# A two-layer graph network on one core: layer 0 in groups of up to eight pairs, its leaks taken from PSUM, its outputs summed by VectorE

## The chip, the core and the metric

The kernel runs on one core of a Trainium2 chip. The metric is the device time of one execution in microseconds (us), and lower is better. Three timed executions of the kernel before gave 8651.25, 8656.15 and 8656.24 us, so the median is 8656.15 us. A further execution was profiled and took 8639.11 us; all views of the profile belong to that one.

## What is computed

There are 12500 nodes with 64 features and 400000 edges, sorted by target. Two graph layers follow one another, each added to its input and normalised over the features:

```python
# layer 0, for every edge (src -> dst)
msg_in = concatenate([x[dst], x[src] - x[dst]], axis=-1)
h = leaky_relu(msg_in @ W1 + b1, 0.01)
h = leaky_relu(h @ W2 + b2, 0.01)
out = segment_sum(h, dst)
x = layernorm(x + out)
# layer 1: attention with 4 heads over the same edges (and self loops):
# softmax over the edges of a target, weighted sum of x[src] @ W, mean of the heads
x = layernorm(x + attention(x))
```

The first product of layer 0 splits: `x[dst] @ (W1a - W1b) + b1` depends on the target alone, and `x[src] @ W1b` on the source alone. Both are made once for every node, and an edge then costs one gathered row, an addition, a leak, a product with W2 and a second leak.

## The kernel before, in words

**Windows.** The nodes are sorted by degree and cut into 98 windows of 128 nodes, one node to a partition. Window w has room for `KW[w]` edges for each of its nodes, from 64 down to 19, 3180 slots in all. Every slot of a window is one indirect DMA issued by GpSimd (POOL), which fetches one table row for each of the 128 nodes: `gather_rows`, line 278. Layer 0 makes 3180 of them from `btab`, layer 1 makes 3180 from `t1tab`.

**Preparation.** Before that, the nodes pass in natural order through eight batches: six of 14 columns, one of 8 and one of 6. For each batch GpSimd gathers edge rows into `rt` (98 gathers, line 278), `Terms` makes the two products of each node and `Bins` counts the degrees. A batch is worked off in groups of up to four columns, and `in_step` (from line 565) writes the order out by hand: for step i it issues `turn` of group i (four PE transposes and a ScalarE copy to `xt`), `mark` of group i of the batch before (VectorE builds the one-hot `oh`, then PE products, line 522 to 529), `multiply` of the same group i (PE, line 498, then a VectorE addition, line 499, and two ScalarE copies, lines 503 and 504), and `place` of group i-1 (VectorE, lines 535 and 537). After the steps VectorE compares the edge rows (`lt`, line 590), reduces them and takes the degrees, which `degrees` also copies by ScalarE and sends out by a DMA of SP. The order of the source is the order on every engine (`manual_schedule`).

**Layer 0.** `fetch0` issues the gathers of window w+2 ahead of the work on window w; the tile `g` that they fill has five buffers. Two slots make a pair, so a window has `KW[w] // 2 + 1` pairs, 1663 in all. They are worked off in groups of up to four pairs, 453 groups, last pairs first. For a group, `expand` transposes the pairs on PE (line 878) into PSUM and VectorE adds the target's term into `ht` in SBUF (line 880). `leak` (line 884) is one VectorE instruction that reads `ht` from SBUF twice, once times 0.01, and keeps the larger. `second` multiplies with W2 (line 889) and ScalarE adds the bias into `t` in SBUF (line 891); `leak` again. `collect` adds the two halves of a pair by a PE product with `both` (line 898), accumulates the groups in PSUM, and VectorE reduces the last four columns (line 903). Then `norm` makes the window's rows and `logits` their attention terms, which SP writes to `t1tab` and `state`. The groups run in a pipeline that is written out: in iteration i the loop issues `second` of group i-2, `expand` and the first leak of group i, the second leak of group i-2, `collect` of group i-4, and `norm` and `logits` one and two iterations after a window's last `collect`.

**Index tables.** For every batch of up to seven windows `index_slots` builds the slot indices on VectorE (lines 249 to 275) out of rows `xab` that GpSimd has gathered.

**Layer 1** gathers from `t1tab`, so its first gather comes after the last window's rows have been written. It is not touched by the change.

The two lines that a sentence does not say exactly:

```python
            def leak(x):
                nc.vector.scalar_tensor_tensor(x, x, 0.01, x, op0=ALU.mult, op1=ALU.max)
```

Of the kernel before, what the change touches and what calls it, by code (L numbers as in the profile page):

```python
# [10 lines left out]
F32 = mybir.dt.float32  # L11
# [10 lines left out]
P = 128  # L22
D = 64
# [3 lines left out]
G = 8  # L27
# [35 lines left out]
def tile_gnn_resnorm(ctx: ExitStack, tc: tile.TileContext, x, src, dst, w1, b1, w2, b2,  # L63
# [397 lines left out]
    with tc.tile_pool(name="prep", bufs=1) as prep, \  # L461
# [19 lines left out]
        class Terms:  # L481
# [10 lines left out]
                nc.scalar.copy(self.xt[:, :n, :], pt[:, :n, :])  # L492

            def multiply(self):
                n, g0, g1 = self.n, self.g0, self.g1
                pab = pps2.tile([P, 4, 2 * D], F32, name="pab")
                for w in range(n):
                    nc.tensor.matmul(pab[:, w, :], self.xt[:, w, :], wab, start=True, stop=True)
                nc.vector.tensor_tensor(
                    self.rt[:, self.o:self.o + n, D:X0].rearrange("p w (a d) -> p w a d", a=2),  # L500
                    pab[:, :n, None, :D].to_broadcast([P, n, 2, D]),
                    b1_bc[:, None, None, :].to_broadcast([P, n, 2, D]), op=ALU.add)
                nc.scalar.copy(bt[0][:, g0:g1, 1:], pab[:, :n, D:])
                nc.scalar.copy(bt[1][:, g0:g1, :D], pab[:, :n, D:])
# [53 lines left out]

        def degrees(a, b):
            nc.vector.tensor_sub(deg[:, a:b], ptr[:, a + 1:b + 1], ptr[:, a:b])  # L560
            nc.scalar.copy(info[:, a:b, 1], deg[:, a:b])
            nc.scalar.copy(info[:, a:b, 2], ptr[:, a:b])
            nc.sync.dma_start(xtab_v[:, a:b, XL:], info[:, a:b, :])
            return [Bins(g, min(g + 4, b)) for g in range(a, b, 4)]

        def in_step(terms, bins):
            for i in range(max(len(terms), len(bins)) + 1):
                if i < len(terms):
                    terms[i].turn()
                if i < len(bins):  # L570
                    bins[i].mark()
                if i < len(terms):
                    terms[i].multiply()
                if 0 <= i - 1 < len(bins):
                    bins[i - 1].place()

        rts = [load_inputs(*batches[0]), load_inputs(*batches[1])]
        nc.vector.tensor_sub(wab[:, :D], w1a, wab[:, D:])
# [122 lines left out]
    with tc.tile_pool(name="l0", bufs=1) as l0:  # L701
# [131 lines left out]

        with tc.tile_pool(name="m0", bufs=2) as mp, \
                tc.tile_pool(name="m0_t", bufs=4) as tp, \
                tc.tile_pool(name="m0_h", bufs=4) as hp, \
                tc.tile_pool(name="m0_x", bufs=3) as xp, \
                tc.tile_pool(name="m0_g", bufs=5) as gp, \
                tc.tile_pool(name="m0_ps", bufs=2, space=PSUM) as mps, \
                tc.manual_schedule():  # L840
            per = G // 2
            raws, own = {}, {}

            def fetch0(w):
                if w in batches:
                    index_slots(mp, *raws[w])
                    own[w] = raws.pop(w)
                else:
                    own[w] = own.pop(w - 1)
                for b in batches[:-1]:  # L850
                    if b not in done and b <= w + 2:
                        done.add(b)
                        raws[b] = load_rows(xp, b)
                k = KW[w]
                xa = own[w][2][:, w - own[w][0], :]

                g = gp.tile([P, KMAX // 2 + 1, 2 * DB], F32, name="g")
                nc.vector.memset(g[:, k // 2, (k % 2) * DB:], 0.0)
                for j in range(k):
                    gather_rows(g[:, j // 2, (j % 2) * DB:(j % 2 + 1) * DB], btab[j % 2],  # L860
                                idx_all[:, KOFF[w] + j:KOFF[w] + j + 1])
                return xa, g
# [9 lines left out]
            def expand(q):  # L872

                g = bufs[q.w][1]
                n, p0 = q.n, q.p0
                q.pt = mps.tile([P, per, P], F32, name="pt0")
                for p in range(p0, p0 + n):
                    nc.tensor.transpose(q.pt[:, p - p0, :], g[:, p, 1:1 + 2 * D], ident)  # L878
                q.h = hp.tile([P, per, P], F32, name="ht")
                nc.vector.tensor_tensor(q.h[:, :n, :], q.pt[:, :n, :],  # L880
                                        terms[q.w][:, None, :].to_broadcast([P, n, P]), op=ALU.add)

            def leak(x):
                nc.vector.scalar_tensor_tensor(x, x, 0.01, x, op0=ALU.mult, op1=ALU.max)  # L884

            def second(q):
                n = q.n
                py = mps.tile([P, per, P], F32, name="py0")
                nc.tensor.matmul(py[:, :n, :], w2_2, q.h[:, :n, :], start=True, stop=True)  # L889
                q.t = hp.tile([P, per, P], F32, name="t0")  # L890
                nc.scalar.activation(q.t[:, :n, :], py[:, :n, :], AF.Identity, bias=b2_col)  # L891

            def collect(q):

                if q.first:
                    sums[q.w] = mps.tile([D, per, P], F32, name="acc0")
                    cts[q.w] = mp.tile([P, P], F32, name="ct")
                nc.tensor.matmul(sums[q.w][:, :q.n, :], both, q.t[:, :q.n, :], start=q.first,  # L898
                                 stop=q.last)
                if q.p0 + q.n == KW[q.w] // 2 + 1:  # L900
                    nc.scalar.copy(cts[q.w][D:, :], q.t[D:, q.n - 1, :])
                if q.last:
                    nc.vector.tensor_reduce(cts[q.w][:D, :],
                                            sums.pop(q.w).rearrange("d j p -> d p j"), AX.X,
                                            ALU.add)

            def norm(w):
                pz = mps.tile([P, P], F32, name="pz", tag="small")
                nc.tensor.transpose(pz, cts.pop(w), ident)  # L909
                xa, g = bufs.pop(w)  # L910

                npad = mp.tile([P, 1], F32, name="npad")
                nc.vector.tensor_scalar(npad, xa[:, XL + 1:XL + 2], float(KW[w]),
                                        float(-2 * (KW[w] // 2 + 1)), op0=ALU.min, op1=ALU.add)
                cn = mp.tile([P, D], F32, name="cn")
                nc.scalar.mul(cn, pz[:, D:], npad)  # L916
                z = mp.tile([P, D], F32, name="z0")
                nc.vector.tensor_add(z, pz[:, :D], cn)
                nc.vector.tensor_add(z, z, xa[:, :D])
                t1 = tp.tile([P, D1], F32, name="t1")  # L920
                layer_norm(mp, z, t1[:, :D])

                for j in range(2):
                    nc.vector.tensor_copy(idx_all[:, KOFF[w] + j:KOFF[w + 1]:2],
                                          g[:, :(KW[w] + 1 - j) // 2, j * (2 * DB - 1)])
                rows[w] = t1
# [19 lines left out]
                               t1[:, None, :D].to_broadcast([P, H, D]))  # L946
                nc.sync.dma_start(state[w * P:(w + 1) * P, :], st)

            bufs, terms, sums, cts, rows, done = {}, {}, {}, {}, {}, set()
            queue = []  # L950
            for w in range(NW):


                pairs = KW[w] // 2 + 1
                qs = [Group(w, p0, min(per, pairs - p0)) for p0 in range(0, pairs, per)]
                assert qs[0].n == per and (pairs % per == 0 or len(qs) > 2)
                qs = qs[::-1]
                if qs[0].n < per and len(qs) > 2:
                    qs[:2] = qs[1::-1]
                qs[0].first = qs[-1].last = True  # L960
                queue += qs
            done.add(0)
# [2 lines left out]
            bufs[1] = fetch0(1)  # L965
            own_term(0)
            late = {}
            for i in range(len(queue) + 7):
                if 0 <= i - 2 < len(queue):
                    second(queue[i - 2])  # L970
                if i < len(queue):
                    q = queue[i]
                    if q.first:
                        if q.w + 2 < NW:
                            bufs[q.w + 2] = fetch0(q.w + 2)
                    expand(q)
                    leak(q.h[:, :q.n, :])
                    if q.last and q.w + 1 < NW:
                        own_term(q.w + 1)
                if 0 <= i - 2 < len(queue):  # L980
                    q = queue[i - 2]
                    leak(q.t[:, :q.n, :])
                if 0 <= i - 4 < len(queue):
                    q = queue[i - 4]
                    collect(q)
                    if q.last:
                        late[i + 1] = (norm, q.w)
                        late[i + 2] = (logits, q.w)
                if i in late:
                    late[i][0](late[i][1])  # L990


        def weights1(pool, g, k, st):
# [260 lines left out]
```

## Time and profile before

| what | value |
|---|---|
| median of three timed executions | 8656.15 us |
| profiled execution, device time | 8639.11 us |
| its span (first to last instruction) | 8637.4 us |
| POOL busy, share of the span | 6381.8 us, 74% |
| VectorE busy, share of the span | 4242.0 us, 49% |
| PE busy, share of the span | 1855.1 us, 21% |
| ScalarE busy, share of the span | 953.0 us, 11% |
| gathers of layer 0: count, mean duration | 3180, 969 ns |
| gathers of layer 1: count, mean duration | 3180, 944 ns |
| pause of POOL between two gathers (most frequent) | 0.30 us |
| POOL idle before the first `xab` gather | 93.5 us |
| POOL idle between the layers, before the first `t1tab` gather | 24.1 us |

The profile lists instructions by source line, engine, operation and tiles, written as out<-in. "Busy" is the time in which an engine executes; the pause in front of an instruction is listed with what ended it. An indirect DMA of GpSimd keeps the engine busy for 940 ns or more, and its data lands 2.4 us (median) after the issue. "issue" is a pause that nothing in the profile explains. The stage view gives the busy time of each engine between two points of the span, with the granted clock of PE (1.00 is full) and the DMA engines' share.

### The profile page before, as it was taken

The page shows a single profiled execution, that of the slowest core. Times are in us where ns is not written, and L with a number is a line of the kernel's source. Part 1 is how long each engine was busy: PE and PEld are TensorE (multiplying, and loading weights), DVE is VectorE, ACT ScalarE, POOL GpSimd, SP SyncE. Part 2 cuts the span into 40 slices and gives each one's busy share as a digit, 9 for nine tenths or more (in the row PEclk, how much of TensorE's full clock was granted, in tenths as well). Part 3 has the DMA queues.
Part 4 walks back from the last instruction along what each step waited for, and adds up shares of the span by engine and source line. Part 5 has one row for each costly group of instructions (what it writes and reads, how often), then busy time and mean ns, then how long its engine had stood idle before and what let it go on. Part 6 is the DMA issues. An engine that isn't in the chain of part 4 may idle for free. (4 is left out here: it accounts for less than half of the span.)

```text
span 8637.4 us, 30329 instructions
## 1 busy us (share of the span) xinstructions
PE 1855.1 (21%) x5401; PEld 816.5 (9%) x5402; DVE 4242.0 (49%) x6604; ACT 953.0 (11%) x2268; POOL 6381.8 (74%) x6668
## 2 busy tenths in 40 slices
PE   4233343433333333333430000000000000000000
PEld 3211111111111111111110000000000000000000
DVE  4432323323323332333325666666666666666667
ACT  2111010111111111111110000000000001101111
POOL 4477777777777777777767777777777777777776
PEclk9766665666666666666665555555555555555555
DMA  6211111111111111111112111111111111111111
GB/s 137 61 33 30 32 31 33 34 31 33 34 31 34 34 35 35 31 35 35 36 33 30 31 31 32 31 32 32 31 32 32 32 32 33 32 33 33 33 33 26
DMA packets 313179, 308.33 MB, mean 36 GB/s; under 512 B 164924, under 2 KB 204331, under 8 KB 312347
## 3 DMA queue, kind: packets, MB, share of 16 engines
q0 software_dynamic: 216064, 242.80, 14.9%
q1 hardware_dynamic: 96632, 61.87, 2.8%
q10 hardware_dynamic: 282, 1.63, 0.1%
q14 instruction: 154, 1.26, 0.0%
q8 instruction: 47, 0.77, 0.0%
HBM read 262.66 MB, written 43.18 MB: 35 GB/s over the span
## 5 line engine op out<-in xcount | busy, mean ns | idle before, releaser
L278 POOL DMA_INDIRECT g<-btab,idx_all x3180 | 3082.6, 969 | 976.0 <-issue 940.2
L278 POOL DMA_INDIRECT g<-t1tab,idx_all x3180 | 3002.9, 944 | 998.8 <-issue 923.8
L880 DVE TENSOR_TENSOR ht<-pt,at 128x512 f32<-128x512 f32 (+3 forms) x453 | 292.8, 646 | 2684.8 <-PE pt L878 2680.6
L1136 DVE TENSOR_REDUCE red<-wx 128x256 f32<-128x4096 f32 (+12 forms) x192 | 1389.3, 7236 | 0.1
L878 PE MATMUL pt<-ident,g 128*128 128x128 f32 x1663 | 404.5, 335 | 2608.2 <-DMA g<-btab,idx_all 2608.0
L1129 DVE TENSOR_TENSOR wx<-g,wt 128x4096 f32<-128x4096 f32 (+12 forms) x192 | 877.0, 4568 | 166.0 <-ACT wt L1108 166.0
L1158 PE MATMUL pn<-ident,nrm 128*128 128x128 f32 x196 | 67.3, 447 | 3911.7 <-DVE nrm L1154 3865.1
L1087 DVE TENSOR_TENSOR lg<-g,ad 128x128 f32<-128x128 f32 (+24 forms) x101 | 29.7, 294 | 1135.1 <-DMA g<-t1tab,idx_all 797.2
L889 PE MATMUL py<-ht,w 128*128 128x512 f32 (+3 forms) x906 | 578.4, 726 | 1.7 <-DVE ht L884 1.7
L898 PE MATMUL acc<-t,both 128*64 128x512 f32 (+3 forms) x906 | 571.6, 720 | 0.0
L878 PEld LDWEIGHTS pt<-ident,g 128*128 128x128 f32 x1663 | 253.1, 164 | 2987.9 <-issue 2852.6
L891 ACT ACTIVATE t<-py,b_col 128x512 f32<-128x512 f32 (+3 forms) x453 | 294.1, 649 | 1145.8 <-PE py L889 1143.8
L1158 PEld LDWEIGHTS pn<-ident,nrm 128*128 128x128 f32 x196 | 28.3, 203 | 3929.9 <-DVE nrm L1154 3709.2
L884 DVE SCALAR_TENSOR_TENSOR ht<-ht 128x512 f32<-128x512 f32 (+3 forms) x453 | 295.1, 651 | 15.5
L1090 ACT ACTIVATE lg_low<-lg 128x128 f32<-128x128 f32 (+24 forms) x101 | 27.8, 275 | 2435.5 <-DVE lg L1087 2435.5
L884 DVE SCALAR_TENSOR_TENSOR t<-t 128x512 f32<-128x512 f32 (+3 forms) x453 | 290.3, 641 | 1.0 <-ACT t L891 0.9
L889 PEld LDWEIGHTS py<-ht,w 128*128 128x128 f32 x906 | 169.1, 232 | 259.4 <-ACT t L891 74.7
L278 POOL DMA_INDIRECT xab<-xtab,node_i x98 | 97.8, 997 | 123.0 <-issue 120.0
L933 ACT COPY x1t<-px 64x128 f32<-64x128 f32 x98 | 25.3, 258 | 1298.2 <-PE px L931 1297.2
L278 POOL DMA_INDIRECT rt<-etab,first_i x98 | 99.8, 1018 | 89.3 <-SPq L400 43.2
L916 ACT ACTIVATE cn<-pz,npad 128x64 f32<-128x64 f32 x98 | 30.7, 313 | 1119.5 <-PE pz L909 1021.3
L283 POOL DMA_INDIRECT out_dram<-o,node_i x98 | 96.7, 987 | 60.0 <-issue 30.8
(209 smaller groups left out, 2686.8 us busy)
## 6 DMA issues: line engine op xcount, KB each, us to landing
g<-btab,idx_all POOLq DMA_INDIRECT x3180, 2.4
g<-t1tab,idx_all POOLq DMA_INDIRECT x3180, 2.4
state<-st SPq DMA_DIRECT2D x98, 134.0 KB
st<-state SPq DMA_DIRECT2D x98, 134.0 KB
xtab<-rt SPq DMA_DIRECT2D x6, 2016.0 KB
btab<-bt SPq DMA_DIRECT2D x2, 3185.0 KB
t1tab<-t SPq DMA_DIRECT2D x98, 34.0 KB
x<-t1tab SPq DMA_DIRECT2D x98, 32.0 KB
```

What stands on the lines that cost most here:

```text
L278: nc.gpsimd.indirect_dma_start(out=o, out_offset=None, in_=table[:, :], in_offset=bass.IndirectOffsetOnAxis(ap=idx, axis=0))
L283: nc.gpsimd.indirect_dma_start(out=table[:, :], out_offset=bass.IndirectOffsetOnAxis(ap=idx, axis=0), in_=i, in_offset=None)
L878: nc.tensor.transpose(q.pt[:, p - p0, :], g[:, p, 1:1 + 2 * D], ident)
L880: nc.vector.tensor_tensor(q.h[:, :n, :], q.pt[:, :n, :], terms[q.w][:, None, :].to_broadcast([P, n, P]), op=ALU.add)
L884: nc.vector.scalar_tensor_tensor(x, x, 0.01, x, op0=ALU.mult, op1=ALU.max)
L889: nc.tensor.matmul(py[:, :n, :], w2_2, q.h[:, :n, :], start=True, stop=True)
L891: nc.scalar.activation(q.t[:, :n, :], py[:, :n, :], AF.Identity, bias=b2_col)
L898: nc.tensor.matmul(sums[q.w][:, :q.n, :], both, q.t[:, :q.n, :], start=q.first, stop=q.last)
L916: nc.scalar.mul(cn, pz[:, D:], npad)
L1129: nc.vector.tensor_tensor(f.wx[:, :n], f.g[:, j0:j0 + n, None, :D].to_broadcast([P, n, H, D]), f.wt[:, j0:j0 + n, :, None].to_broadcast([P ...
L1136: nc.vector.tensor_reduce(red.rearrange("p h d -> p (h d)"), f.wx[:, :n].rearrange("p k h d -> p (h d) k"), AX.X, ALU.add)
L1158: nc.tensor.transpose(pn[:, j, :], f.nrm[:, 2 * j:2 * j + 2, :], ident)
```

## The change

It has four parts, all before layer 1.

1. Layer 0's groups hold up to eight pairs instead of four. Both leaks read PSUM: VectorE adds the target's term in place in PSUM, ScalarE writes 0.01 times that into SBUF (`low0`), and VectorE takes the larger of the two into `ht`. After the second product ScalarE writes 0.01 times (product plus bias) into SBUF (`low1`), and VectorE adds the bias to the product in PSUM and takes the larger. The product with `both` is gone: all outputs of a window stay in one SBUF tile, VectorE sums them over the pairs in one reduction of 128 rows, and `norm` transposes two tiles and adds the halves.
2. The buffers change: `g` has four instead of five, the second product's PSUM tile has one, the index work has one.
3. The order of layer 0's loop changes: the pipeline is two iterations long (one for the last four groups), and the last window's pairs are taken in ascending order.
4. In the preparation, `multiply` is split into the PE products and a `store` with the VectorE addition and ScalarE copies. In step i, the products of group i-1 are issued ahead of `turn` and `mark` of group i, and `store` of group i-1 comes last. The copies and the DMA of the degrees move behind the first step.

The core of the diff:

```diff
             def multiply(self):
-                n, g0, g1 = self.n, self.g0, self.g1
+                n = self.n
...
+                self.pab = pab
+
+            def store(self):
+                n, g0, g1, pab = self.n, self.g0, self.g1, self.pab
                 nc.vector.tensor_tensor(
...
         def in_step(terms, bins):
             for i in range(max(len(terms), len(bins)) + 1):
+                if 0 <= i - 1 < len(terms):
+                    terms[i - 1].multiply()
                 if i < len(terms):
                     terms[i].turn()
                 if i < len(bins):
                     bins[i].mark()
-                if i < len(terms):
-                    terms[i].multiply()
                 if 0 <= i - 1 < len(bins):
                     bins[i - 1].place()
+                if 0 <= i - 1 < len(terms):
+                    terms[i - 1].store()
+                if i == 0 and bins:
+                    store_info(bins[0].g0, bins[-1].g1)
...
-                tc.tile_pool(name="m0_g", bufs=5) as gp, \
+                tc.tile_pool(name="m0_g", bufs=4) as gp, \
...
             def expand(q):
...
-                q.h = hp.tile([P, per, P], F32, name="ht")
-                nc.vector.tensor_tensor(q.h[:, :n, :], q.pt[:, :n, :],
-                                        terms[q.w][:, None, :].to_broadcast([P, n, P]), op=ALU.add)
-
-            def leak(x):
-                nc.vector.scalar_tensor_tensor(x, x, 0.01, x, op0=ALU.mult, op1=ALU.max)
+                nc.vector.tensor_tensor(q.pt[:, :n, :], q.pt[:, :n, :],
+                                        terms[q.w][:, None, :].to_broadcast([P, n, P]), op=ALU.add)
+                q.low = lp.tile([P, per, P], F32, name="low0")
+                nc.scalar.mul(q.low[:, :n, :], q.pt[:, :n, :], 0.01)
+
+            def leak(q):
+                n = q.n
+                q.h = hp.tile([P, per, P], F32, name="ht")
+                nc.vector.tensor_tensor(q.h[:, :n, :], q.pt[:, :n, :], q.low[:, :n, :], op=ALU.max)

             def second(q):
...
-                q.t = hp.tile([P, per, P], F32, name="t0")
-                nc.scalar.activation(q.t[:, :n, :], py[:, :n, :], AF.Identity, bias=b2_col)
+                low = lp.tile([P, per, P], F32, name="low1")
+                nc.scalar.activation(low[:, :n, :], py[:, :n, :], AF.Identity, bias=b2_low,
+                                     scale=0.01)
+                nc.vector.scalar_tensor_tensor(outs[q.w][:, p0:p0 + n, :], py[:, :n, :], b2_col,
+                                               low[:, :n, :], op0=ALU.add, op1=ALU.max)
...
-                nc.tensor.matmul(sums[q.w][:, :q.n, :], both, q.t[:, :q.n, :], start=q.first,
-                                 stop=q.last)
...
+                nc.vector.tensor_reduce(sums[w], t[:, :n, :].rearrange("d j p -> d p j"), AX.X,
+                                        ALU.add)
...
-                qs = qs[::-1]
-                if qs[0].n < per and len(qs) > 2:
-                    qs[:2] = qs[1::-1]
+                if w < NW - 1:
+                    qs = qs[::-1]
...
+            at = [i + (2 if i < len(queue) - 4 else 1) for i in range(len(queue))]
+            for i in range(len(queue) + 3):
+                for f, w in late.pop(i, ()):
+                    f(w)
+                if 0 <= i - 1 < len(queue):
+                    leak(queue[i - 1])
+                now = [q for q, k in zip(queue, at) if k == i]
                 if i < len(queue):
...
                     expand(q)
...
+                for q in now:
+                    second(q)
                     if q.last:
-                        late[i + 1] = (norm, q.w)
-                        late[i + 2] = (logits, q.w)
+                        collect(q.w)
+                        late.setdefault(i + 1, []).append((norm, q.w))
+                        late.setdefault(i + 2, []).append((logits, q.w))
```

## The prediction

> **What bounds the kernel now.** I read the page first: how full each engine is, and whether one is full throughout.
>
> ```profile
> POOL 4477777777777777777767777777777777777776
> ...
> L278 POOL DMA_INDIRECT g<-btab,idx_all x3180 | 3082.6, 969 | 976.0 <-issue 940.2
> L278 POOL DMA_INDIRECT g<-t1tab,idx_all x3180 | 3002.9, 944 | 998.8 <-issue 923.8
> L880 DVE TENSOR_TENSOR ht<-pt,at 128x512 f32<-128x512 f32 (+3 forms) x453 | 292.8, 646 | 2684.8 <-PE pt L878 2680.6
> ...
> L884 DVE SCALAR_TENSOR_TENSOR ht<-ht 128x512 f32<-128x512 f32 (+3 forms) x453 | 295.1, 651 | 15.5
> ```
>
> POOL is at seven tenths in nearly every slice, and its gathers explain it: 0.944 us of work, then 0.305 us that ends by "issue", 1.25 us in all, 6360 times. VectorE waits 2680 us for PE, and PE for gathers. So in both layers only POOL's own pace counts: a saving on VectorE, PE or ScalarE by itself is worth nothing there. But the two kinds of gather do the same work, and layer 0's take 969 ns against 944: 79.7 us in all. The stages say where else POOL stands still:
>
> ```profile
> 46.00:192.00 146.00, 78.86 (x384) 60.60 (x385) 72.94 (x124) 34.27 (x95) 99.71 (x98) 1.00 0.76 147
> 192.00:285.00 93.00, 57.70 (x435) 48.81 (x434) 66.06 (x140) 39.34 (x133) 0.00 (x0) 1.00 0.42 119
> ...
> 296.00:4471.00 4175.00, 1523.13 (x3926) 579.63 (x3926) 1316.64 (x3497) 471.90 (x1213) 3177.22 (x3275) 0.63 0.17 33
> 4471.00:4496.00 25.00, 14.95 (x39) 5.24 (x38) 13.00 (x49) 7.37 (x24) 0.90 (x2) 0.77 0.10 25
> ```
>
> The fifth pair of figures behind the colon is POOL. From 192 to 285 us it has nothing: preparation is behind, and its chain is the path. From 4471 to 4496 it waits for the last window's rows. Three places, then: long gathers in layer 0, the preparation's chain, the change of layers.
>
> **Part 1, the leaks.** The timeline shows what makes a gather long:
>
> ```profile
> 4442.54 0.69 DVE L880 TENSOR_TENSOR ht<-pt,at 128x512 f32<-128x512 f32 x1 [8.78 <-PE pt L878]
> 4443.26 0.69 DVE L884 SCALAR_TENSOR_TENSOR ht<-ht 128x512 f32<-128x512 f32 x1
> 4443.34 1.44 POOL L278 DMA_INDIRECT g<-btab,idx_all  x1 [0.31 <-issue]
> 4443.87 0.68 DVE L884 SCALAR_TENSOR_TENSOR t<-t 128x512 f32<-128x512 f32 x1
> ```
>
> The gather that runs beside the leaks takes 1.44 us; those beside nothing take 0.94. I went through all gathers of the layer (3275 with `xab`) and sorted them by what VectorE did meanwhile. 793 have a leak beside them: together 67.6 us over 0.944 each. 198 have only the slot arithmetic (lines 254 to 265, two inputs in SBUF): 19.4 us. The other 2284: -1.0 us. The common feature is two SBUF inputs, not VectorE being busy: 177 gathers had only line 880 beside them (PSUM and SBUF) and average -0.4 ns, at most +5; 43 had only the second leak beside them and average +112, at most +431. Layer 1's gathers have line 1129 (SBUF and PSUM, 683 gathers alone, -0.4 ns) and the reduction of line 1136 (one SBUF input, 938 alone, -0.3 ns) beside them all the time.
>
> After the change the four instructions that a group has on VectorE or shares in (addition, maximum, addition with maximum, reduction) have at most one tensor from SBUF. All 906 leaks with two go; the slot arithmetic stays. Gain: 67 us; bounds 55 (the slot arithmetic, shifted, meets more gathers) and 79.7 (the whole difference to layer 1).
>
> [...]
>
> What lies beside: VectorE goes from 1317 us to about 1600 in the layer (three passes of some 290 us as in lines 880 and 884, a reduction of 1663 x 128 columns at line 1136's 1.7 ns each = 363 us, the rest as before), ScalarE gets one more pass (+290 us), PE loses `collect` (572 us). None comes near 4100 us, so the larger groups and the single PSUM buffer cost nothing. If that cover were gone, POOL would wait. Four buffers of `g`: the gathers of window w+2 start when those of w+1 are issued and need `norm` of w-2, which the new order puts behind the last groups of w-1 or the first of w, a whole window (24 us at the least) earlier. Index slots are likewise made two windows ahead. Cost: nothing, bounds 0 to 3 us.
>
> **Part 2, the preparation.** VectorE's timeline in a batch:
>
> ```profile
> 161.99 0.69 DVE L499 TENSOR_TENSOR rt<-pab,b_bc 128x512 f32<-128x512 f32 x1 [3.20 <-PE pab L498]
> 162.60 0.68 DVE L535 TENSOR_TENSOR sel<-pr,oh 128x512 f32<-128x512 f32 x1
> 163.32 0.69 DVE L537 TENSOR_REDUCE rank<-sel 128x4 f32<-128x512 f32 x1
> 163.92 0.15 DVE L514 SCALAR_TENSOR_TENSOR key<-deg,spare_k 128x4 bf16<-128x4 f32 x1
> 164.11 0.69 DVE L517 TENSOR_TENSOR oh<-key,col_k 128x512 bf16<-128x512 bf16 x1
> 167.99 0.69 DVE L499 TENSOR_TENSOR rt<-pab,b_bc 128x512 f32<-128x512 f32 x1 [3.19 <-PE pab L498]
> ```
>
> A step is a ring: 2.8 us of VectorE, then 3.2 us for PE's `mark` products and the `multiply` queued behind them, 6.0 us. The new order breaks it: PE multiplies group i-1, turns group i and marks it, while VectorE places and stores group i-1 beside it. PE then sets the step: 2.0 us for `multiply` (159.88 to 161.89), 0.85 for four transposes, 1.02 for `mark` (164.86 to 165.88): 3.9 us, 3.0 for a short group. VectorE needs 2.8 and is covered.
>
> A batch of 14 runs now from comparison to comparison in 27.3 us (120.32 to 147.65). New: 7.55 from the comparison to the end of the first `mark` (147.65 to 155.20, unchanged), 3.9 + 3.9 + 3.0, then 1.25 for the last short `multiply` and 0.42 for its addition: 20.0 us. That saves 7.3 us in each of the batches 2 to 6; the first has no bins and waits for gathers. The same count gives 4.0 and 3.7 us for the two small batches. Sum: 44 us. What is late next: the gathers of a batch need 14 x 1.25 us plus about 1.4 us for the one beside the comparison, 18.9 us, just less than 20.0. POOL's own wait for an `rt` buffer (15.3 us at 184.6) goes too, and is not counted, since the chain is later than it. On SP, the DMA of the degrees now comes behind the next batch's load; both land in the batch's time. Between 237 and 285 us nothing changes. I take 42 us, for DMAs that get less room (0.76 of the engines' time already); bounds 25 and 46.
>
> **Part 3, the change of layers.** The last gather ends at 4471.3, its data meets PE at 4473.6, and the first `t1tab` gather follows at 4495.4. Behind 4473.6 the new order has: transposes 0.4, addition 0.7, ScalarE 0.7, wait for the group before it 3.5 (its 768 columns pass PE, ScalarE and VectorE first), maximum 0.7, product 1.5, ScalarE 0.7, addition with maximum 0.7, reduction of 1280 columns 2.2, two transposes 0.5, three additions 0.7, and 5.4 from the normalisation to the gather (4490.07 to 4495.44, unchanged): 17.7 us, against 21.8. Gain 4 us, bounds 0 and 8.
>
> **Sum.** 67 + 42 + 4 = 113 us. The profiled execution took 8639.1 us, 1.7 more than its span, so it should take 8526. The median of the timed runs lies 17 us higher; with the same difference it comes to **8543 us**.
>
> **Rivals.**
> - *The DMA engines set the preparation's pace.* For: 0.76 of their time is used, and the stores and loads of a batch are packed closer. At 21 to 25 us of DMA time per batch, a batch might not go under 24 us: 3.5 us saved five times and 7.7 at the end, 25 us instead of 44. Against: gathers keep their pace there. Time: 8562 us. Chance 12%.
> - [...] Chance 8%.
> - *The window's sum holds POOL up.* It is one reduction of some 3.7 us (363/98), SBUF to SBUF, where line 1136 writes PSUM. If it held gathers as `lt` (line 590, 2.03 us, two SBUF inputs) does, whose neighbours took 2.3 to 2.55 us, the cost would be its length less 0.6, 3.1 us each, 304 us: 8847 us, slower. It decides from 113/98 = 1.15 us per window. Against: the reduction of line 593, SBUF to SBUF, had 4 gathers alone beside it, at +1.2 ns. Chance 4%.
>
> **Numbers.** The forecast has 76%. Its own terms reach from 8522 (79.7 + 46 + 8) to 8579 (55 + 25 + 0, less 3). With the first rival inside and some room for the runs' spread, the range is 8520 to 8590; the other two rivals stay out. A measurement can tell about 0.2% (17 us) from no change. Faster 94%, same 2%, slower 4%.
>
> **What will show it.** Right: layer 0's gathers at 950 ns on average; comparisons 20 us apart in the preparation, and the first `xab` gather near 243 us instead of 285; about 20 us between the layers. Wrong: gathers longer than 0.95 us beside the maximum or the window's sum; pauses of POOL in layer 0 longer than 0.31 us that a VectorE or PE instruction ends; comparisons still 24 us or more apart.

## The result and the profile after

The changed kernel takes **8547.55 us** (median of four runs, 8546.79 to 8548.33). The kernel before took 8654.52 us beside it (8651.25 to 8656.24). The difference is 107.0 us; the ratio is 0.9877, with a 95% interval of 0.9860 to 0.9894. The profiled execution took 8547.6 us, 91.5 us less than that of before.

First the page after, by its slices and its groups:

```profile
POOL 4677777777777777777767777777777777777776
...
L278 POOL DMA_INDIRECT g<-t1tab,idx_all x3180 | 3010.3, 947 | 1003.7 <-issue 923.6
L278 POOL DMA_INDIRECT g<-btab,idx_all x3180 | 3025.7, 951 | 976.6 <-issue 944.6
...
L926 DVE TENSOR_REDUCE ts<-t 128x128 f32<-128x2176 f32 (+13 forms) x98 | 371.0, 3785 | 3.4
...
L904 DVE TENSOR_TENSOR ht<-pt,low 128x1024 f32<-128x1024 f32 (+4 forms) x251 | 259.1, 1032 | 1.5 <-ACT low L899 1.5
```

Layer 0's gathers take 951 ns instead of 969, while those of layer 1, which the change does not touch, take 947 instead of 944. POOL's idle time ahead of layer 0's gathers is the same as before (976.6 against 976.0 us), so larger groups, fewer buffers and VectorE's longer sums made no gather wait. The stages:

```profile
46.00:185.00 139.00, 92.83 (x472) 73.68 (x473) 93.79 (x158) 41.77 (x115) 101.70 (x98) 1.00 0.94 175
185.00:243.00 58.00, 41.19 (x347) 36.16 (x346) 46.44 (x106) 31.61 (x113) 0.40 (x1) 1.00 0.38 140
...
254.00:4367.00 4113.00, 1155.67 (x3132) 619.73 (x3133) 1580.30 (x2997) 556.15 (x1072) 3114.76 (x3275) 0.59 0.17 33
4367.00:4396.00 29.00, 10.79 (x25) 5.07 (x23) 14.54 (x37) 5.92 (x18) 0.36 (x2) 0.50 0.08 20
```

The preparation is shorter: the first `xab` gather starts at 242.6 us instead of 285.3. Its DMA engines are now busy for 0.94 of the time instead of 0.76. The last row is longer, not shorter: POOL stands still for 28.6 us between the layers instead of 24.1, and the clock granted to PE (the third figure from the end) is 0.50 there, where it was 0.77. So the 91.5 us are 42.7 from the preparation and 61.2 from the stretch of layer 0, less 4.5 at the change of layers and 7.9 in layer 1. The last 7.9 are no doing of the change, which leaves layer 1 as it was: undisturbed gathers of this execution take 947 ns in both layers, 3 ns more than in the execution profiled before, and 3180 x 3 ns = 9.5 us.

### The profile page after: what moved, and what is told of

Read it like the earlier page. It is cut to its first block, busy times and chain, and to the rows that moved or that the text cites. A ratio compares the mean times of both kernels' runs of the same rounds, so it can differ in the third digit from the quotient of the medians.

```text
span 8545.8 us, 28395 instructions
## 1 busy us (share of the span) xinstructions
PE 1480.9 (17%) x4593; PEld 857.0 (10%) x4594; DVE 4508.8 (53%) x6096; ACT 1035.7 (12%) x2121; POOL 6330.4 (74%) x6668
## 3 DMA queue, kind: packets, MB, share of 16 engines
q14 instruction: 152, 1.25, 0.0%
## 5 line engine op out<-in xcount | busy, mean ns | idle before, releaser
L278 POOL DMA_INDIRECT g<-btab,idx_all x3180 | 3025.7, 951 | 976.6 <-issue 944.6
L896 DVE TENSOR_TENSOR pt<-pt,at 128x1024 f32<-128x1024 f32 (+4 forms) x251 | 262.0, 1044 | 1749.4 <-PE pt L895 1749.4
L895 PE MATMUL pt<-ident,g 128*128 128x128 f32 x1663 | 462.9, 400 | 2037.0 <-DMA g<-btab,idx_all 2035.8
L1111 DVE TENSOR_TENSOR lg<-g,ad 128x128 f32<-128x128 f32 (+24 forms) x101 | 29.7, 294 | 1143.1 <-DMA g<-t1tab,idx_all 824.5
L918 DVE SCALAR_TENSOR_TENSOR t<-py,b_col,low 128x1024 f32<-128x1024 f32 (+4 forms) x251 | 276.2, 1101 | 632.0 <-ACT low L916 632.0
L899 ACT ACTIVATE low<-pt 128x1024 f32<-128x1024 f32 (+4 forms) x251 | 220.3, 878 | 2683.8 <-DVE pt L896 2683.8
L926 DVE TENSOR_REDUCE ts<-t 128x128 f32<-128x2176 f32 (+13 forms) x98 | 371.0, 3785 | 3.4
L913 PEld LDWEIGHTS py<-ht,w 128*128 128x128 f32 x906 | 235.9, 291 | 261.2 <-issue 172.8
L916 ACT ACTIVATE low<-py,b_low 128x1024 f32<-128x1024 f32 (+4 forms) x251 | 243.9, 972 | 138.9 <-PE py L913 138.6
L904 DVE TENSOR_TENSOR ht<-pt,low 128x1024 f32<-128x1024 f32 (+4 forms) x251 | 259.1, 1032 | 1.5 <-ACT low L899 1.5
L297 ACT ACTIVATE ln_sd<-ln_mv,eps_t 128x1 f32<-128x1 f32 x196 | 57.7, 294 | 1123.8 <-DVE ln_mv L295 1123.8
```

The lines of the kernel that those rows point to most:

```text
L278: nc.gpsimd.indirect_dma_start(out=o, out_offset=None, in_=table[:, :], in_offset=bass.IndirectOffsetOnAxis(ap=idx, axis=0))
L896: nc.vector.tensor_tensor(q.pt[:, :n, :], q.pt[:, :n, :], terms[q.w][:, None, :].to_broadcast([P, n, P]), op=ALU.add)
L899: nc.scalar.mul(q.low[:, :n, :], q.pt[:, :n, :], 0.01)
L904: nc.vector.tensor_tensor(q.h[:, :n, :], q.pt[:, :n, :], q.low[:, :n, :], op=ALU.max)
L913: nc.tensor.matmul(py[:, p:p + m, :], w2_2, q.h[:, p:p + m, :], start=True, stop=True)
L916: nc.scalar.activation(low[:, :n, :], py[:, :n, :], AF.Identity, bias=b2_low, scale=0.01)
```

## The experiments

Three series ran, each on one chip with the kernel before beside it. Labels e1 to e12 are the runs. The undisturbed gather (the median one) took 944 or 945 ns in the first two series, 947 in the profile of after, so times are compared inside a series. "Pause" below is the time from the last gather of layer 0 to the first of layer 1. "Excess" below is the time of layer 0's 3180 gathers of `btab` over the median of that run. It is 80.7 us in before and 14.2 us in after.

### The kernel before once more (e1), and the two halves of the change (e2, e4)

e1 is the kernel before, unchanged.

> The kernel before, unchanged, profiled again. The profiled execution of before took 8639.1 us with undisturbed gathers of 944 ns, the timed ones 8651 to 8656 us; the profile of the changed kernel has undisturbed gathers of 947 ns. Theory: POOL's pace differs by 3 ns a gather between executions or chips, and 6556 indirect DMAs times 3 ns are the 17 us; then this profile shows either 944 ns and about 8639 us, or 947 ns and about 8656 us, and nothing that mixes the two. Rival: profiling as such is 17 us faster for this kernel; then 944 ns and 8639 us again, beside timed runs of 8655 us on the same chip.

It took 8640.23 us, ratio 0.9998 (0.9988 to 1.0008). The profiled execution took 8646.52 us with gathers of 945 ns, while the timed ones took 8637.58 to 8642.99: profiling as such does not make this kernel 17 us faster, so the rival is refuted. The theory's two cases were not met exactly, but its price was: 1 ns more than 944 on each of 6556 indirect DMAs is 6.6 us, and 8639.1 + 6.6 = 8645.7.

e2 is the kernel before with the new preparation alone: `multiply` and `store` split, the new order in `in_step`, the degrees' copies behind the first step. Its layer 0 is the old one.

> The kernel before with the new order of the preparation alone. Theory: the ring of VectorE and PE set the batches, so comparisons come 20 us apart instead of 27, the first xab gather comes 43 us earlier, and nothing else moves: about 8612 us. Rival: part of the 43 us in the changed kernel comes from something else (buffers, the other pools), or the DMA engines give it back: 8625 us or more.

8603.57 us against 8642.26, ratio 0.9957 (0.9940 to 0.9973): 38.7 us less. The first `xab` gather starts at 249.1 us, 37.0 earlier than in e1. Excess 74.6 us (79.6 in e1), pause between the layers 24.8 us (25.0): little else moved.

e4 keeps the old preparation, groups of four, the old loop and `collect`, and takes only the new form of the two leaks:

```diff
-                nc.vector.tensor_tensor(q.h[:, :n, :], q.pt[:, :n, :],
+                nc.vector.tensor_tensor(q.pt[:, :n, :], q.pt[:, :n, :],
                                         terms[q.w][:, None, :].to_broadcast([P, n, P]), op=ALU.add)
+                nc.scalar.mul(q.low[:, :n, :], q.pt[:, :n, :], 0.01)
...
-                nc.vector.scalar_tensor_tensor(x, x, 0.01, x, op0=ALU.mult, op1=ALU.max)
+                nc.vector.tensor_tensor(q.h[:, :n, :], q.pt[:, :n, :], q.low[:, :n, :], op=ALU.max)
```

> The kernel before with only the leaks changed: addition in place in PSUM, 0.01 times by ScalarE, maximum of PSUM and SBUF; groups of four, the product with both, the loop and the preparation as before. Theory: layer 0's gathers fall to 950 ns on average and the time by 67 us, to about 8588 us (8583 to 8598). Rival (the larger groups or the window's sum bring it): 8655 us, gathers at 969 ns.

8583.63 us, ratio 0.9932 (0.9916 to 0.9949): 58.6 us less. The gathers in e1 and then in e4:

```profile
L278 POOL DMA_INDIRECT g<-btab,idx_all x3180 | 3084.7, 970 | 975.9 <-issue 948.5
```

```profile
L278 POOL DMA_INDIRECT g<-btab,idx_all x3180 | 3023.2, 951 | 975.9 <-issue 952.1
```

The excess is 18.1 us instead of 79.6. Its pause between the layers is 30.0 us instead of 25.0. The two halves give 38.7 + 58.6 = 97.3 us; the whole change with an added instruction that costs nothing (e8, below) gives 97.7 on the second chip. So, as far as two chips can be set side by side, no gain is left for the larger groups, the new loop and VectorE's sums.

### The old leaks in the new loop (e3)

```diff
-                nc.vector.tensor_tensor(q.h[:, :n, :], q.pt[:, :n, :], q.low[:, :n, :], op=ALU.max)
+                x = q.h[:, :q.n, :]
+                nc.vector.scalar_tensor_tensor(x, x, 0.01, x, op0=ALU.mult, op1=ALU.max)
...
-                nc.vector.scalar_tensor_tensor(outs[q.w][:, p0:p0 + n, :], py[:, :n, :], b2_col,
-                                               low[:, :n, :], op0=ALU.add, op1=ALU.max)
+                t = outs[q.w][:, p0:p0 + n, :]
+                nc.scalar.activation(t, py[:, :n, :], AF.Identity, bias=b2_col)
+                nc.vector.scalar_tensor_tensor(t, t, 0.01, t, op0=ALU.mult, op1=ALU.max)
```

> The changed kernel with both leaks put back to one VectorE instruction that reads the same SBUF tile twice; the groups of eight, the window's sum, the loop and the preparation stay. Theory (two SBUF inputs hold up POOL's gathers): layer 0's gathers go back to 965 to 985 ns on average, 60 to 110 us more than the changed kernel (the instructions are fewer but up to 1.1 us long): 8610 to 8660 us. [...]

8684.65 us, ratio 1.0054 (1.0037 to 1.0071): slower than before, in spite of the new preparation. The form of the leaks is what counts. But the size was unexpected. Its row of gathers:

```profile
L278 POOL DMA_INDIRECT g<-btab,idx_all x3180 | 3158.4, 993 | 976.1 <-issue 954.5
```

The excess is 156.5 us, twice that of before, although the leaks keep VectorE busy for less time (521 us in 502 instructions against 585 us in 906). Its timeline, VectorE and POOL, shows why:

```profile
2999.90 1.23 DVE L914 SCALAR_TENSOR_TENSOR t<-t 128x1024 f32<-128x1024 f32 x1
3000.32 1.62 POOL L278 DMA_INDIRECT g<-btab,idx_all  x1 [0.30 <-issue]
...
3035.25 0.94 POOL L278 DMA_INDIRECT g<-btab,idx_all  x1 [0.30 <-issue]
...
3035.40 1.23 DVE L914 SCALAR_TENSOR_TENSOR t<-t 128x1024 f32<-128x1024 f32 x1
...
3036.50 0.94 POOL L278 DMA_INDIRECT g<-btab,idx_all  x1 [0.30 <-issue]
```

The gather at 3000.32 starts while a leak runs. The leak ends at 3001.13, the gather at 3001.94. The gather at 3035.25 starts 0.15 us ahead of a leak that then covers all the rest of it, and it is not held at all. The one at 3036.50 starts 0.13 us before that leak ends: no loss. I put this to all gathers of layer 0. Those held by more than 30 ns are 325 in before, 379 in e3, 250 in e7 (below) and 84 in after, and every one of them started while a VectorE instruction with two inputs in SBUF was running. With the loss taken as that instruction's end, less the gather's start, less 0.13 us (0.14 in e3), if it already runs 0.04 us (0.02 in e3) ahead of the start (these allowances were fitted to the runs), the sums are 78.0, 154.2, 86.5 and 17.8 us, against excesses of 80.7, 156.5, 86.1 and 14.2 (17.9 for the 84 held ones alone). Gather by gather the correlation is 0.93, 0.98, 0.99 and 1.00. By this fit, an estimate, an instruction twice as long is met twice as often at a gather's start and holds it more than twice as long: the cost grows faster than its length (excess 80.7 us in before with leaks of 0.65 us, 156.5 in e3 with leaks of 1.04). The leaks themselves are not held by the gathers: 72 of e3's second leaks of 1024 columns start while a gather runs and take 1.23 us on average, and so do the 56 others.

### A needless instruction, with and without two inputs in SBUF (e7, e8)

Both add one VectorE instruction per group to the changed kernel, of the same shape and length, whose output is not used. e7 reads SBUF twice, e8 PSUM and SBUF:

```diff
                 nc.vector.tensor_tensor(q.h[:, :n, :], q.pt[:, :n, :], q.low[:, :n, :], op=ALU.max)
+                extra = lp.tile([P, per, P], F32, name="extra")
+                nc.vector.tensor_tensor(extra[:, :n, :], q.low[:, :n, :], q.low[:, :n, :], op=ALU.max)
```

In e8 the first input is `q.pt[:, :n, :]`.

> The changed kernel with one more VectorE instruction per group, a maximum of up to 128x1024 with both inputs from SBUF, written to a tile that nobody reads. 251 instructions of about 1.1 us, all hidden as far as VectorE goes. Theory (two SBUF inputs): each lengthens a gather beside it; 906 leaks of 0.65 us cost 67 us, that is 0.075 us each, and with the square of the length 0.2 us each: 50 us (30 to 120) more than the changed kernel. [...]

> The same extra instruction with one input from PSUM and one from SBUF. Theory: 0 within 5 us, 8548 us, gathers at 951 ns. Rival (any further VectorE work beside the gathers costs): as much as with two SBUF inputs.

The gathers and the added instruction in e7 and then in e8:

```profile
L278 POOL DMA_INDIRECT g<-btab,idx_all x3180 | 3088.0, 971 | 976.2 <-issue 953.9
...
L906 DVE TENSOR_TENSOR extra<-low 128x1024 f32<-128x1024 f32 (+4 forms) x251 | 259.6, 1034 | 0.0
```

```profile
L278 POOL DMA_INDIRECT g<-btab,idx_all x3180 | 3019.8, 950 | 976.2 <-issue 952.4
...
L906 DVE TENSOR_TENSOR extra<-pt,low 128x1024 f32<-128x1024 f32 (+4 forms) x251 | 258.6, 1030 | 0.0
```

251 instructions, 1.03 us each in both, cost 8615.46 - 8538.76 = 76.7 us when both inputs are in SBUF, 0.31 us apiece, and nothing that can be measured when one is in PSUM (gathers of 950 ns, 951 in after; e7: ratio 0.9975, 0.9966 to 0.9985; e8: 0.9888, 0.9872 to 0.9905). The edits differ in nothing else, so this settles the first part. In e7 it is a tensor_tensor that holds the gathers (971 ns on average, 950 in e8). What in a gather is held, no run shows.

### The change of layers (e5, e6)

After's timeline of that stretch, VectorE alone. The last data land at about 4369.7.

```profile
4369.16 1.15 DVE L918 SCALAR_TENSOR_TENSOR t<-py,b_col,low 128x896 f32<-128x896 f32 x1 [3.67 <-ACT low L916]
4370.34 2.51 DVE L926 TENSOR_REDUCE ts<-t 128x128 f32<-128x1408 f32 x1
...
4375.93 0.95 DVE L904 TENSOR_TENSOR ht<-pt,low 128x768 f32<-128x768 f32 x1
4376.80 0.69 DVE L896 TENSOR_TENSOR pt<-pt,at 128x512 f32<-128x512 f32 x1
...
4386.72 2.30 DVE L926 TENSOR_REDUCE ts<-t 128x128 f32<-128x1280 f32 x1
```

The reduction of 1408 columns at 4370.34 is the sum of window 96, the last but one: it is still to be done when the last window's data are there. Behind it come that window's norm and the maximum of the last window's first group, and only at 4376.80 the addition of its last four pairs, 7 us after their data. Two edits try to take this away. They are about the lag: in the changed loop a group's second product comes two iterations behind its first. In e5 the last two windows go without the lag, each finished before the next begins. In e6 the last three windows have groups of four, with one iteration of lag for the last six groups.

```diff
+            ends = [q for q in queue if q.w >= NW - 2]
+            queue = queue[:len(queue) - len(ends)]
             at = [i + (2 if i < len(queue) - 4 else 1) for i in range(len(queue))]
...
+            for w in range(NW - 2, NW):
+                qs = [q for q in ends if q.w == w]
...
+                collect(w)
+                norm(w)
+                logits(w)
```

```diff
                     n = left if left <= per else per if left >= per + BANK else left - BANK
+                    if w >= NW - 3:
+                        n = min(n, BANK)
...
-            at = [i + (2 if i < len(queue) - 4 else 1) for i in range(len(queue))]
+            at = [i + (2 if i < len(queue) - 6 else 1) for i in range(len(queue))]
```

> The changed kernel, but the loop finishes window 95 wholly before it touches window 96, and the last two windows are worked off one after the other without the two-iteration lag (the groups and their sizes stay). In the changed kernel 28.6 us pass between the last gather of layer 0 and the first of layer 1, where the prediction had 20 and the kernel before 24.1. Theory (the lag holds the second product of window 95 until the data of window 96 are there, so that three windows' work stands in a row behind it): the pause falls to 19 to 21 us, the time to about 8539 us. Rival (the chain of one group of eight is long by itself, and the lag does not matter): the pause stays at 26 to 29 us and the time at 8547 us.

> The changed kernel with groups of at most four pairs in the last three windows; the lag of the loop stays, one iteration for the last six groups. Theory (the lag and what stands behind it): no gain over 3 us, the pause at 26 to 30 us. Rival (the size of the groups): the pause falls to 20 us, the time to 8539 us.

e5: 8539.40 us, ratio 0.9889 (0.9872 to 0.9905), pause 29.7 us. e6: 8537.72 us, ratio 0.9886 (0.9869 to 0.9902), pause 28.6 us. Neither gained: e8, whose added instruction costs nothing, took 8538.76 us in this series with a pause of 27.6 us. So e5's theory is refuted. In e5 the work is handed on all the same, as its timeline shows:

```profile
4363.20 2.51 DVE L926 TENSOR_REDUCE ts<-t 128x128 f32<-128x1408 f32 x1
...
4371.70 0.97 DVE L896 TENSOR_TENSOR pt<-pt,at 128x768 f32<-128x768 f32 x1 [0.85 <-PE pt L895]
```

Window 96 is through by 4370, but window 97's first six pairs are turned and added only then, although their data landed at about 4359 (its last data at 4367, less seven gathers of 1.25 us). Window 96 itself began only at 4350, behind window 95, though its last gather had ended at 4341.4. Window 95's smaller group was added at 4318.3, 3 us after its last gather had ended, but its larger one only at 4330.6, behind the rest of window 94.

Time is also lost in e4, with the old loop and groups of four: e1 and e4 differ in the form of the leaks alone, and the pause goes from 25.0 to 30.0 us. The last product and the last column product in e1, and then in e4:

```profile
4484.35 1.12 PE L889 MATMUL py<-ht,w 128*128 128x512 f32 x2
...
4490.41 1.36 PE L898 MATMUL acc<-t,both 128*64 128x512 f32 x2
```

```profile
4420.23 2.08 PE L893 MATMUL py<-ht,w 128*128 128x512 f32 x2
...
4427.54 1.97 PE L910 MATMUL acc<-t,both 128*64 128x512 f32 x2
```

The same products take 2.08 and 1.97 us in e4 where they take 1.12 and 1.36 in e1. Seven of PE's instructions in this end are longer in e4, by 3.9 us together, not all of it on the chain; its pause is 5.0 us longer. The granted clock over the pause is 0.77 in e1, 0.67 in e4 and 0.50 in after, where the last product of 512 columns takes 2.04 us again. The same product thus has two durations, 1.12 and 2.08 us, and the longer one stands beside the lower clock. That the ScalarE step which e4 adds between the two products lowers the clock was the author's guess; no run changed it alone. And it cannot be the only cause: e3, the new loop with the old leaks, has the clock of 0.50 over the pause too, and its last product of 512 columns takes 2.05 us. Its pause is 26.8 us, so the new leaks cost 5.0 us here in the old loop (e1 to e4) and 1.8 in the new one (e3 to after).

### The last series (e9 to e12)

The last series ran on the chip of the first, but in it every kernel, the kernel before too, took 10.0 to 10.3 ms instead of 8.6, so its numbers cannot be set beside the others. e9 is the changed kernel itself. e10 removes the lag for the last eight windows, as e5 does for two. e11 takes the difference and the product of the slot arithmetic in PSUM, with groups of four to make room. e12 does both.

```diff
-            nc.vector.tensor_tensor(dif, cur[:, :, s:s + width], cur[:, :, 0:width],
+            nc.vector.tensor_tensor(d, cur[:, :, s:s + width], cur[:, :, 0:width],
                                     op=ALU.subtract)
-            nc.vector.tensor_tensor(dif, dif, bit[:, :, None].to_broadcast([P, nw, width]),
+            nc.vector.tensor_tensor(d, d, bit[:, :, None].to_broadcast([P, nw, width]),
                                     op=ALU.mult)
-            nc.vector.tensor_tensor(dif, dif, cur[:, :, 0:width], op=ALU.add)
+            nc.vector.tensor_tensor(dif, d, cur[:, :, 0:width], op=ALU.add)
```

> The changed kernel once more, unchanged, as the measure for the three beside it, on a chip where the kernel before runs too. If the saving of the preparation depends on how far the DMA engines set its pace, the first row of xtab is gathered between 242 us (the profile of after) and 250 us (e5, e6 and e8, which have the same preparation), and the comparisons start 20.4 to 22.5 us apart. If what was seen there is the edits of e5, e6 and e8 after all, it is 242 to 243 us again. The pause between the layers is 28 to 29 us by every theory, and the time 0.987 to 0.989 of before.

> The last eight windows are taken without the lag of two iterations: each window's groups go through both orders and its norm before the next window's first transpose. In e5 only the last two went so, and window 95 still began 6 us after its own data had landed, because half of window 94 lay in front of it. Theory 1, the work handed down from window to window is what makes the pause longer: a window's chain takes 20 us in e5 (4350 to 4370), its gathers 27 us, so the 6 us are gone after one window, window 96 begins with its data, the last one's first group is in work before the last data land, and the pause is 21 to 25 us instead of 28.6, the time 4 to 7 us less than that of after on this chip. Theory 2, the last window's own chain of one group of six and one of four pairs is what takes the time, whatever lies in front of it: the pause stays at 27 to 30 us, the time within 3 us of after.

> In the changed kernel the slot arithmetic of each batch (lines 254 to 265) takes its difference and product in PSUM, so that of its three operations only the last one has both inputs in SBUF; to make room in PSUM the groups are of four pairs again. The gathers that lay beside these operations hold the 14 to 18 us that the gathers of btab in after still take over their undisturbed pace. If operations with two inputs in SBUF are what holds a gather, about two thirds of that goes: an excess of 5 to 9 us, the time 6 to 12 us less than after on this chip, less what groups of four cost at the change of layers (0 to 2 us). If it is the mass of VectorE's work, whatever its inputs, the excess stays at 14 to 18 us and the time within 3 us of after.

> Both of the two edits before in one kernel. If both theories hold, the gains add up: 10 to 18 us less than after on this chip, a pause of 20 to 25 us and an excess of 5 to 9 us. If only one holds, the time of that one alone.

(Of the three operations in e11 it is the first, not the last, that still has both inputs in SBUF. And in the text on e10 the window that began 6 us after its data is 96; window 95's first addition came 3 us after its last gather.) Before took 10091.75 us there, e9 10029.65 (ratio 0.9949, 0.9931 to 0.9968), e10 10073.39 (0.9985, 0.9969 to 1.0000), e11 10212.52 (1.0131, 1.0112 to 1.0150), e12 10261.56 (1.0179, 1.0162 to 1.0196). None of the four came out as expected: e9's first `xab` gather is at 288 us and its pause 46.6 us, and the other three are slower than e9. The gathers of e9:

```profile
L278 POOL DMA_INDIRECT g<-btab,idx_all x3180 | 3005.8, 945 | 1913.9 <-issue 1789.4
L278 POOL DMA_INDIRECT g<-t1tab,idx_all x3180 | 3363.4, 1058 | 1122.4 <-issue 1040.8
```

Layer 0's gathers are undisturbed in themselves, but POOL waits 1914 us ahead of them instead of 977. 58 pauses between its gathers are longer than 2 us and come to 955 us together (none in after); the one at 2031, 10.8 us long, ends when VectorE has made the slot indices. VectorE is late there because it gets PE's results late: over the whole layer ScalarE reads a second product 7.8 us (median) after the start of its last matmul, against 1.1 in after. The records show nearly the same clock as after's (0.55 against 0.56), the same 400 ns for a transpose and 906 ns for a second product's matmul against 821, so what held the results up is not in the trace; and as layer 1, with little work for PE, has longer gathers too, PE cannot be all of it.

What these runs say is little. With groups of four e11 takes 183 us more than e9, and without the lag the pause of e10 is 80.0 us against 46.6: where PE is late, lag and large groups seem to be a cover that they are not elsewhere. In e11 not one of the 3180 gathers of `btab` is held by more than 30 ns, in e9 16 are. That fits the operands, but POOL's gathers met VectorE differently there. Whether e10 or e11 gain anything where before takes 8.6 ms stays open.

## Why the prediction was right, and where it was not

**The leaks: 67 us predicted, 71.6 found.** The excess of layer 0's gathers, `xab` included, fell from 85.9 to 14.3 us; e4 alone gives 61.5 of `btab`'s. The cause, two inputs in SBUF, is shown by e7 and e8, and e3 and e4 agree. The prediction went by its own rows of gathers, and that choice was right. What it did not have is the condition: the instruction must be running when the gather starts, as it was for all 325 held gathers in before, 379 in e3, 250 in e7 and 84 in after. It did not need it, as all of the leaks go.

**The cover in layer 0: nothing predicted, nothing found.** POOL's idle time ahead of the gathers is unchanged, and e2 and e4 add up to the whole. The loads beside it were right for VectorE (1580 us against about 1600) and off for ScalarE (84 us more against 290) and PE (367 us less against 572), which cost nothing here, as neither engine is near full.

**The window's sum (third rival): refuted.** 215 gathers of after had the sum of line 926 alone beside them: 945.7 ns on average, at most 962, where 947 is undisturbed. **The long gathers stay (second rival, 8%): refuted** by layer 0's row of 951 ns in after, 969 in before. No run shows anything that its 8%, and with it the 76%, could rest on; what the runs showed in its place is that the operands matter (gathers of 971 ns in e7, 950 in e8).

**The preparation: 42 us predicted, 42.7 found in this execution, 37.0 in e2.** In after, VectorE's steps of one batch are these:

```profile
126.96 2.02 DVE L602 TENSOR_TENSOR lt<-rt,node_f 128x1792 bf16<-128x1792 uint16 x1 [0.63 <-DMA rt<-etab,first_i]
...
136.61 0.69 DVE L503 TENSOR_TENSOR rt<-pab,b_bc 128x512 f32<-128x512 f32 x1 [1.06 <-PE pab L498]
...
140.53 0.69 DVE L503 TENSOR_TENSOR rt<-pab,b_bc 128x512 f32<-128x512 f32 x1 [1.10 <-PE pab L498]
...
147.60 2.03 DVE L602 TENSOR_TENSOR lt<-rt,node_f 128x1792 bf16<-128x1792 uint16 x1 [0.43 <-DMA rt<-etab,first_i]
```

A step takes 3.92 us (predicted 3.9), a batch 20.64 (predicted 20.0). The wait ahead of the comparison ends with a gather's landing, as "what is late next" had it. This is where the first rival is partly true. VectorE's waits in the preparation of after, and then of e8, whose preparation is the same code:

```profile
DVE lt L602 <- DMA rt<-etab,first_i: 2.0, 3, 0.9
```

```profile
DVE lt L602 <- DMA rt<-etab,first_i: 7.1, 5, 2.7
```

There the comparison waits 7.1 us for gathers instead of 2.0, POOL itself waits 15.6 us for earlier gathers' landings instead of 6.7, the DMA engines are busy for 0.97 of the time from 46 to 192 us (0.92 in after, 0.76 in before), and the first `xab` gather comes at 248.8 us. So waits for gathers now share in setting the pace, at a price of 5 to 9 us in the first two series (first `xab` gather at 247.7 to 251.1 us) where the rival put 19. That the nearly full DMA engines are why these gathers land late is an inference from the two profiles.

**The change of layers: a gain of 4 us predicted (bounds 0 and 8), a loss of 4.5 found. This step failed.** It counted the chain behind the last data as if VectorE had only the last window left. It holds window 96 too: the addition of the last group starts 6.7 us later than the 0.4 us behind the data that the step has. The kernel before has such work too, inside its 21.8 us (window 96's norm starts at 4475.53, ahead of the addition of the last window's last group at 4478.46), and the new sum left it out. And it took 1.5 us for the product of 512 columns, which takes 2.04; PE's clock is lower in this stretch (0.50) than in the kernel before (0.77). The 8.6 us between 17.7 predicted and 26.3 measured are thus 6.7 of inherited work and 1.9 along the chain itself. That the inherited work is the cause was argued from the timeline; with the two edits meant to remove it the pause stayed, and e4 loses 5.0 us without the new loop. So the cause stays open.

**The sum.** 113 us were predicted; 71.6 + 42.7 - 4.5 = 109.8 were found in the profiles, and the timed runs differ by 107.0. In the profiled execution 3 ns on each of 6360 gathers, 19 us, hide part of it: it took 8547.6 us where 8526 was expected, while the timed runs agree with it. The 17 us that stood between profiled and timed runs before were carried over, and did not recur: two misses of like size, of opposite sign, brought the 8543 so close to 8547.55. They may be one thing, the pace of the gathers, counted twice: 944 ns in the profile of before, 947 in that of after. The timed runs of before left no profile, so this is not shown. In the second series the change, in e8's form, is worth 97.7 us, where its first `xab` gather comes 6 us later than in after; the gain is not the same from series to series.

## What to carry to other kernels

Where GpSimd's gathers set the pace, look at what VectorE runs at the moment a gather starts: here an instruction with both inputs in SBUF held it until about its own end (a gather of e3 took 1.62 us instead of 0.94 where 0.81 us of such a leak were left), so put one operand in PSUM (251 added instructions cost 76.7 us more in e7, with both in SBUF, than in e8, with one in PSUM), and if that can't be, make such instructions short rather than few (906 leaks of 0.65 us went with an excess of 80.7 us here, 502 of 1.04 with 156.5). An engine that is idle for 60% of a layer can still be behind at the layer's end, as VectorE was here (busy for 1580 us of 4113, its last addition 7 us behind the data): count what it has inherited, and how long PE's products take there, before a chain is counted from the last data on. Where the same kernel is profiled and timed, compare the undisturbed duration of the commonest instruction first; 3 ns on 6360 of them were 19 us here.

## What the runs showed of the hardware

- A gather of 128 rows (944 ns undisturbed) that was held by more than 30 ns had always started while VectorE ran an instruction with two inputs in SBUF (325, 379, 250 and 84 gathers in four runs), and was held by about as much as was then left of that instruction, less 0.13 us: with 0.81 us left it took 1.62 us. That is a wait until the end, not a slowdown in proportion: a gather of e3 that started 0.15 us ahead of such an instruction, with the instruction beside it for all the rest, took 0.94 us.
- The undisturbed gather took 944 (before), 945 (e1) or 947 ns (after), the same in both layers of an execution and different between executions (the last series apart): 19 us for the kernel.
- In the last series the same kernel took 10030 us, with PE's results read 7 us later (median) and layer 1's gathers at 1058 ns on average, at nearly the same recorded clock of PE (0.55 against 0.56).
